# A two-layer graph kernel on one core: other orders for the first and last pairs, one load moved to another queue, filler products at the end left out

## The chip, the cores and the metric

The kernel runs on one core of one Trainium2 chip. A core has five engines, each with its own instruction stream: TensorE (PE in the profile, its weight loads apart as PEld), VectorE (DVE), ScalarE (ACT), GpSimd (POOL) and SyncE (SP, which here only issues DMAs). The metric is the device time in microseconds; less is better. Before the change the median of three runs is 2414.87 us (2414.79 to 2415.64).

## The reference

128 graphs of 128 nodes with 512 features each. Layer 0 is masked attention with 8 heads of 64, layer 1 a graph attention with one head; each is added to its input and layer-normalised. All in float32.

```python
# layer 0
q, k, v = x @ Wq + bq, x @ Wk + bk, x @ Wv + bv          # 8 heads of 64
logits = einsum('bqhd,bkhd->bhqk', q, k) / 8
attn = softmax(where(adj > 0, logits, -1e9), axis=-1)
x = layernorm(x + relu(einsum('bhqk,bkhd->bqhd', attn, v) @ Wo + bo))
# layer 1
Wh = x @ W
e = leaky_relu((Wh @ a1)[:, :, None] + (Wh @ a2)[:, None, :], 0.2)
x = layernorm(x + elu(softmax(where(adj == 0, -1e9, e), axis=2) @ Wh))
```

## The kernel before

Two graphs are worked on together, a pair; there are 64 pairs, 0 to 63. A pair's work is cut into some 130 steps. Each step is a small function that issues one to eight instructions, mostly on one engine, and has a key: `qk0`, `mask_logits1`, `edge_row`. A last digit 0 or 1 is the graph within the pair (or, for products, the number of the product). In this text a key with a point and a pair is one step: `qk2.1` is the step qk2 of pair 1.

The order of everything is written out by a plan. `PLAN` gives each key a due time, `PERIOD` (78.77) is added for each pair, and `ENDS` gives the first and last pairs shifts of their own on top; the units are the plan's own. `at` (in the main function) puts each step into a list with that sum, the list is sorted, and the steps are issued in this order. So a due time is no time on the chip: it only decides the place of a step's instructions in each engine's stream. An engine works its stream in order; a semaphore holds an instruction until its data are there or its buffer is free. The middle pairs have no shifts and so all have one order.

What the steps of a pair do, by stage:

- Loads, all on SP: `load_blocks` (x in a block form, four DMAs, two buffers), `load_x` (x once more for the residual, three buffers), `load_adj`. `x_transpose` (DVE) makes xT.
- Queries and keys, values, output and second-layer weights are each multiplied by a two-by-two block scheme with 7 products instead of 8: `qk0` to `qk6` (sixteen matmul rows of the profile each), `v0`..., `o0`..., `w0`... (four rows each). It needs sums of blocks: of the weights once at the start (`sums_qk`, `sums_v` on DVE, `sums_o`, `sums_w` on POOL), of the left side for each pair (`x_sums`, `o_sums`, `z_sums` on POOL). The products go to the three PSUM banks A, B and C, one buffer each, and several products are added up in one bank. Between two such products other engines read the bank: `_p1`, `_p1q`, `_c11` (ACT mostly) read A; `_p6`, `_p7`, `_c21` (DVE) read B; `_c22`, `_c12` (DVE) read C. The next product into a bank must wait for the read.
- Attention: `logits` (PE), `fill_logits` (POOL memset), `mask_logits`, `max_logits` (DVE), `exp_logits` (ACT, eight activations), `sum_logits` (DVE), `norm_logits` (ACT, eight), `weights_t` (DVE), then a turn through HBM: `weights_out` (tensor prd) and `weights_in` (prT), `mix_values` (PE, tile po), `mix_values_out` (ACT).
- First norm: `residual0x`, `stats0x`, `mean0x` (DVE), `rstd0x`, `shift0x` (POOL), `norm0x` (ACT).
- Second layer: `edge_termsx` and `edge_blocks` (DVE), `edge_row` (four DMAs, tile ejr), `edge_sums` (ACT), `edge_leaky`, `edge_mask`, `edge_max` (DVE), `edge_exp` (ACT), `edges_t` (DVE) and through HBM with `edges_t_out`, `edges_t_in` (tile attT), `mix_nodes` (PE, tile pz), `mix_nodes_out` (ACT), the w products, `elu_exp` (ACT), `elu_low` (POOL), `elu_max` (DVE), `residual1x` (POOL), the second norm, `store`.

The tiles po, pz, and the transposes named below share one PSUM buffer of tag "ps".

At the start, `a` (1024 numbers) is folded into W, since the second layer needs only W@a1 and W@a2. `fold_a(i)` (keys `sums_fold1`, `sums_fold0`) first issues a DMA on POOL's queue which spreads its half of `a` over all partitions, then does eight DVE multiplications with sums; `fold_t` (PE, tile pwa) transposes the result and `fold_out` (ACT) takes it out. Pair 0 does its queries and keys by plain products, `qk_plain`, since the weight sums aren't ready.

The last pair has no later work to overlap with. It turns its attention weights on PE, does its o and w products plainly from rows of the weights that are loaded again (`rows_o`, `rows_w`, into the buffers of the left sums), and does on DVE what POOL does elsewhere.

Products of zeros, or of the identity, that nobody reads keep PE at work: `keep_going` (12 at the very start) and `keep_going_late`, which `at` puts behind the steps named in `GOING`.

```python
GOING = {('o3', -1): 6, ('mix_nodes0', -2): 2, ('w3', -2): 5, ('w5', -2): 10, ('edges_t', -1): 3, ('mix_nodes1', -1): 1}
shift = ENDS.get(p if p < n_pair // 2 else p - n_pair, {}).get(key, 0.0)
events.append((p * PERIOD + PLAN[key] + shift, len(events), fn, args))
```

Of the kernel before, what the change touches and what calls it, by code (L numbers as in the profile page):

```python
# [8 lines left out]
F32 = mybir.dt.float32  # L9
# [10 lines left out]
    load_adj=-214.2762, load_blocks=-156.4567, sums_qk=-119.9046, x_transpose0=-118.9579, sums_v=-112.8775,  # L20
    x_transpose1=-64.055, sums_fold1=-60.5833, sums_fold_t1=-41.0724, sums_fold0=-37.6761, sums_fold_out1=-36.5398,
    qk0=-36.0224, x_sums=-35.8404, qk1=-32.9779, qk_p1=-31.7105, fill_logits0=-31.5232, sums_fold_t0=-29.2377,
    qk4=-28.6459, qk_p6=-28.5331, qk_p1q=-27.7049, qk2=-26.3155, qk_c11=-24.8916, qk3=-22.6254, v0=-21.402,
    qk_p7=-19.9439, qk_c22=-19.9339, qk5=-14.7467, qk6=-13.4439, qk_c21=-7.8856, qk_c12=-7.8498, v_p1=-4.7268,
    v1=-4.5449, fill_logits1=-1.8505, mask=-1.2435, v_p6=-0.2943, logits=0.0, sums_fold_out0=0.6684,
    mask_logits0=1.9952, max_logits0=3.7429, v3=4.4065, v_p7=4.433, v2=7.4467, v_c11=9.2069, v4=9.2085,
    mask_logits1=10.0374, load_x1=10.3213, v5=13.2871, v_c22=14.6665, exp_logits0=14.7511, v_c21=15.0921,
    v6=17.2266, v_c12=17.5754, max_logits1=22.1216, sums_o=22.3895, sum_logits0=24.0633, norm_logits0=27.409,
    exp_logits1=33.3029, weights_t0=43.7048, sum_logits1=43.7767, norm_logits1=52.0118, weights_out0=53.6197,
    weights_t1=55.6065, weights_out1=68.011, weights_in0=70.4393, weights_in1=74.301, mix_values0=75.8522,  # L30
    mix_values_out0=80.7212, mix_values1=81.4334, mix_values_out1=85.4398, load_x0=87.1711, sums_w=90.2554,
    o_sums=101.6394, o0=106.2181, o_p1=113.6365, o1=113.6652, o4=115.875, o_p6=116.2192, o_p1l=117.1503,
    o3=117.1603, o_p7=117.3205, o2=117.7709, o_c11=118.2449, o_c22=118.2872, o5=120.8539, o6=121.6955,
    o_c21=121.8792, residual01=122.7569, o_c12=122.7614, stats01=122.8191, mean01=123.8502, residual00=127.7304,
    rstd01=128.2803, shift01=128.7729, stats00=130.3078, norm01=131.2371, mean00=131.4538, rstd00=133.9815,
    edge_term01=134.3884, shift00=135.5918, edge_term11=137.3863, norm00=140.4496, edge_term10=144.2793,
    edge_blocks=146.1519, fill_edges=152.9599, edge_row=155.4786, edge_term00=159.9559, edge_sums=163.3873,
    edge_leaky=169.0665, edge_mask=174.9959, edge_max=179.2956, edge_exp=184.846, edges_t=185.9311,
    edges_t_out=188.282, edges_t_in=189.7663, mix_nodes1=211.95, mix_nodes_out1=218.2462, mix_nodes0=220.5122,
    mix_nodes_out0=222.7905, z_sums=231.0565, w0=248.2279, edge_norm=250.3865, w_p1=253.8429, w1=254.0225,  # L40
    w2=254.7456, w_p6=256.7486, w3=258.7144, w_c11=259.1252, w4=262.9461, w_p7=264.5461, w5=268.1992,
    w_c22=268.2862, w6=268.4953, w_c21=269.0061, w_c12=270.9016, elu_exp1=288.3615, elu_exp0=298.9658,
    elu_low1=307.1177, elu_max1=314.1197, elu_low0=326.1878, elu_max0=338.6625, residual10=340.2052,
    stats10=349.6362, mean10=349.9591, residual11=350.8328, rstd10=358.934, stats11=386.2458, mean11=395.8811,
    shift10=413.3316, rstd11=414.603, shift11=416.7025, finish0=436.5642, finish1=440.8676, store0=451.5942,
    store1=492.1186, tail_exp=492.2186, tail_max=492.3186, tail_sum=492.4186, tail_norm=492.5186)
# [3 lines left out]
        qk_p1=-693.3008, qk_p1q=-562.1962, qk_p6=-558.7086, qk0=-497.8592, x_transpose1=-494.0942,  # L50
        x_transpose0=-448.1221, fill_logits0=-367.3107, load_x1=-359.65, qk1=-335.4701, qk2=-331.5901,
        load_adj=-316.9328, load_blocks=-299.7933, qk_c11=-289.6601, tail_max=-280.732, mask=-257.6647, qk3=-220.34,
        fill_logits1=-212.9934, qk_c21=-211.3615, fill_edges=-182.6923, qk_c12=-180.0174, x_sums=-178.1562,
        logits=-170.7364, qk_c22=-165.6554, load_x0=-157.2757, qk5=-129.4956, exp_logits0=-115.2104,
        weights_out0=-114.1682, max_logits0=-113.2581, mask_logits1=-111.564, mask_logits0=-111.5243, v4=-108.9856,
        weights_t0=-107.8966, weights_in0=-106.3568, v1=-104.9602, v3=-103.5122, v_p6=-102.5092,
        sum_logits0=-99.1902, v_p1=-98.6495, v2=-98.1896, v_c22=-97.279, v_p7=-96.9685, v6=-95.93,
        max_logits1=-92.4852, v_c11=-92.0931, norm_logits0=-91.8454, v5=-91.0373, weights_t1=-89.8414, v0=-89.7163,
        norm_logits1=-87.923, sum_logits1=-87.4384, v_c12=-84.3643, exp_logits1=-84.0508, v_c21=-82.1213,
        weights_in1=-81.3671, weights_out1=-75.5973, mix_values0=-73.0572, o_sums=-72.5018,  # L60
        mix_values_out0=-71.3249, stats11=-70.0451, mix_values_out1=-68.3664, o0=-68.2642, mix_values1=-65.5116,
        o_p1l=-63.5095, o1=-61.1023, o_p1=-60.89, qk_p7=-54.0233, mean11=-52.6597, o2=-52.1908, o_p6=-51.8324,
        o3=-51.3338, o5=-49.9351, o_p7=-47.5345, o_c11=-46.8, o_c22=-46.5822, o6=-46.5728, residual11=-45.7167,
        o4=-45.2658, o_c21=-41.1905, store1=-37.7402, residual01=-37.493, elu_low0=-36.3281, residual00=-34.7161,
        stats01=-31.1527, stats00=-30.3568, o_c12=-30.2986, elu_low1=-29.8226, elu_exp0=-28.3417,
        edge_term10=-25.0922, norm00=-23.3134, mean00=-22.364, elu_exp1=-20.4366, elu_max1=-19.6739,
        shift00=-19.0277, rstd00=-18.0188, edge_max=-12.5663, edge_mask=-9.2627, edge_norm=-8.9206, mean01=-8.3685,
        w4=-8.2022, shift01=-8.0908, rstd01=-7.6618, mix_nodes1=-7.0678, edges_t=-6.1798, edge_exp=-5.696,
        edge_term00=-5.0867, edges_t_out=-4.9358, edge_leaky=-4.1925, mix_nodes0=-3.6711, mix_nodes_out1=-3.3264,
        w_c22=-2.764, w5=-2.6295, w6=-2.2085, w_p1=-1.9921, w_c21=-1.864, mix_nodes_out0=-1.4624, w_c12=-0.5349,  # L70
        w_p7=-0.4357, w1=-0.3674, edge_sums=-0.3649, finish1=-0.2784, edge_row=0.4769, w_p6=1.2165,
        edge_blocks=1.691, w_c11=1.7828, w3=2.1516, w0=2.4355, w2=2.5822, elu_max0=4.042, rstd11=4.5885,
        edge_term11=7.4074, norm01=8.5979, shift10=10.18, residual10=10.2246, edge_term01=10.4225, z_sums=13.5305,
        qk4=14.4327, edges_t_in=14.663, shift11=23.8601, stats10=33.5595, finish0=35.2453, store0=36.1082,
        rstd10=37.0667, mean10=39.7004, tail_exp=66.8184, tail_norm=66.9674, tail_sum=88.0048, qk6=88.4639),
    1: dict(
        tail_norm=-490.1808, tail_max=-153.045, load_x1=-116.7791, qk_p1q=-113.1873, qk0=-111.5532, qk_p1=-110.0434,
        qk4=-107.6095, qk2=-106.2391, qk3=-105.0977, x_sums=-102.7439, qk1=-102.1183, fill_logits0=-100.8075,
        qk_p6=-100.3165, qk_c11=-99.2056, qk_p7=-95.9145, v0=-95.2879, x_transpose1=-94.0568, v_p1=-93.2182,
        fill_logits1=-91.2167, qk5=-91.0325, qk_c22=-87.7854, qk_c21=-86.0555, mask=-83.9068, qk6=-74.9886,  # L80
        qk_c12=-72.8526, v1=-72.8444, max_logits1=-71.4972, v_p6=-70.6212, v4=-66.8154, v2=-66.3646,
        logits=-65.0664, mask_logits0=-65.0249, mask_logits1=-64.5572, v3=-63.432, exp_logits1=-63.0166,
        max_logits0=-62.096, v_c22=-61.3606, v_c11=-59.6449, v5=-58.7736, v_p7=-55.6045, elu_max0=-48.704,
        v6=-46.8286, v_c21=-46.2548, sum_logits0=-46.1168, residual10=-45.9116, elu_low0=-45.8965,
        exp_logits0=-45.0705, norm_logits0=-44.0432, v_c12=-37.6454, weights_in0=-36.7489, edge_norm=-35.6444,
        weights_t0=-34.4351, norm_logits1=-31.9896, x_transpose0=-30.4421, sum_logits1=-28.0582,
        weights_in1=-26.5576, weights_out1=-25.0926, o_p1l=-24.9338, o_p1=-23.9869, weights_out0=-23.5663,
        weights_t1=-23.4312, o2=-22.2075, mean11=-20.5856, o_sums=-20.3084, store1=-19.9954, elu_exp0=-19.6693,
        o3=-19.0271, o0=-18.871, o1=-18.228, o_p6=-18.1951, stats11=-17.7549, o_c11=-16.1903, load_x0=-16.0355,
# [153 lines left out]
def tile_two_graph_layers(ctx: ExitStack, tc: tile.TileContext, x, adj, wq, bq, wk, bk, wv, bv, wo, bo, w, a, out,  # L243
# [8 lines left out]
    nc = tc.nc  # L252
# [831 lines left out]
```

## Time and profile before

| | us |
|---|---|
| median of three runs | 2414.87 |
| the profiled execution | 2416.63 |
| its span, first to last instruction | 2414.8 |
| PE busy in the span | 2379.1 |
| one pair in the middle (from one qk step to the same of the next pair) | 36.73 |
| first qk product starts | 7.28 |
| `qk0.4` starts | 140.45 |
| last o product ends | 2376.7 |
| last matmul ends | 2406.8 |

The granted PE clock is 0.998 of full speed over the whole span. The sum of the changes is made against the profiled execution, 1.76 us above the median of the runs.

In a row of the timeline the numbers are start and duration in microseconds, then engine, line, operation, output<-inputs with the number of partitions and elements, a count, and in brackets the engine's idle time before the row with what ended it. In a row of waits: the total, how many, and the longest.

### The profile page before, as it was taken

The page shows a single profiled execution, that of the slowest core. Times are in us where ns is not written, and L with a number is a line of the kernel's source. Part 1 is how long each engine was busy: PE and PEld are TensorE (multiplying, and loading weights), DVE is VectorE, ACT ScalarE, POOL GpSimd, SP SyncE. Part 2 cuts the span into 40 slices and gives each one's busy share as a digit, 9 for nine tenths or more (in the row PEclk, how much of TensorE's full clock was granted, in tenths as well). Part 3 has the DMA queues.
Part 4 walks back from the last instruction along what each step waited for, and adds up shares of the span by engine and source line. Part 5 has one row for each costly group of instructions (what it writes and reads, how often), then busy time and mean ns, then how long its engine had stood idle before and what let it go on. Part 6 is the DMA issues. An engine that isn't in the chain of part 4 may idle for free.

```text
span 2414.8 us, 51884 instructions
## 1 busy us (share of the span) xinstructions
PE 2379.1 (99%) x17768; PEld 2147.7 (89%) x17768; DVE 1859.3 (77%) x3883; ACT 1557.8 (65%) x5512; POOL 1414.3 (59%) x1990
## 2 busy tenths in 40 slices
PE   8999999999999999999999999999999999999997
PEld 7889989989899899899899898998998998998885
DVE  5777777877877877777777778778778777777776
ACT  4656766766766666666667667666666666676664
POOL 3446665655556565665656555565566656555557
PEclk9999999999999999999999999999999999999999
DMA  8435445344344444454443443444444544534333
GB/s 194 114 67 130 112 105 131 101 118 123 104 123 116 112 123 115 101 134 109 108 132 101 117 123 103 123 117 112 123 115 101 134 110 108 134 98 116 109 85 81
DMA packets 341382, 276.59 MB, mean 115 GB/s; under 512 B 126400, under 2 KB 288960, under 8 KB 341120
## 3 DMA queue, kind: packets, MB, share of 16 engines
q1 hardware_dynamic: 339568, 271.17, 43.7%
q8 instruction: 142, 2.33, 0.4%
q10 hardware_dynamic: 1216, 1.31, 0.3%
q0 software_dynamic: 336, 0.79, 0.2%
q14 instruction: 120, 0.98, 0.1%
HBM read 156.90 MB, written 107.87 MB: 110 GB/s over the span
## 4 chain that ended last, share of the span: by engine, by line
PE 92%; DMA 3%; DVE 2%; ACT 2%; SPq 1%; issue 0%; POOL 0%; POOLq 0%; ACTq 0%; DVEq 0%
PE pBqk L486 14%; PE pCqk L486 9%; PE pAqk L486 9%; PE pBv L475 7%; PE pBo L475 7%; PE pBw L475 7%; PE po L804 5%; PE s L731 5%; PE pAo L475 4%; PE pz L914 4%; PE pCw L475 4%; PE pCo L475 4%; PE pAv L475 4%; PE pCv L475 4%; PE pAw L475 4%; DMA ejr<-ej 1%
## 5 line engine op out<-in xcount | busy, mean ns | idle before, releaser
L754 ACT ACTIVATE pr<-pr,nmax 128x128 f32<-128x128 f32 x1024 | 395.3, 390 | 4.0 <-DVE nmax L748 4.0
L763 ACT ACTIVATE pr<-pr,tot 128x128 f32<-128x128 f32 x1024 | 314.5, 411 | 49.8 <-DVE tot L758 49.6
L813 ACT ACTIVATE oT<-po,bv 128x128 f32<-128x128 f32 x512 | 145.0, 364 | 286.0 <-PE po L804 286.0
L956 POOL TENSOR_TENSOR cw<-cw,co 128x512 f32<-128x512 f32 x126 | 159.5, 1285 | 227.1 <-DVE cw L950 227.1
L513 POOL TENSOR_SCALAR rstd<-mv 128x1 f32<-128x1 f32 x255 | 97.6, 383 | 270.4 <-DVE mv L508 261.1
L945 POOL TENSOR_SCALAR t<-t 128x512 f32<-128x512 f32 x126 | 246.9, 1960 | 13.2 <-ACT t L941 13.1
L486 PE MATMUL pBqk<-sx,wqk 128*128 128x128 f32 x2016 | 245.6, 275 | 0.5 <-DVE tot L758 0.5
L486 PE MATMUL pCqk<-sx,wqk 128*128 128x128 f32 x2016 | 246.0, 275 | 0.0
L486 PE MATMUL pAqk<-xT,wqk 128*128 128x128 f32 x2016 | 245.5, 275 | 0.0
L486 PEld LDWEIGHTS pBqk<-sx,wqk 128*128 128x128 f32 x2016 | 239.8, 192 | 3.8 <-issue 0.6
L486 PEld LDWEIGHTS pAqk<-xT,wqk 128*128 128x128 f32 x2016 | 236.3, 192 | 7.0
L486 PEld LDWEIGHTS pCqk<-sx,wqk 128*128 128x128 f32 x2016 | 235.9, 192 | 0.2
L739 POOL MEMSET pr<- 128x1024 f32 x128 | 121.8, 953 | 134.4 <-DVE prb L773 129.8
L743 DVE COPY_PREDICATED pr<-mask,s 128x1024 f32<-128x1024 int32 x128 | 171.0, 1337 | 33.7 <-PE s L731 32.5
L835 DVE SCALAR_TENSOR_TENSOR scr<-co,wa_bc 128x512 f32<-128x512 f32 x256 | 186.3, 728 | 11.3 <-ACT co L523 5.7
L754 ACT ACTIVATION_READ_ACCUMULATOR pr<-pr,nmax 128x1 f32 x1024 | 193.8, 189 | 0.0
L773 DVE STREAM_TRANSPOSE prb<-pr 128x1024 f32<-128x1024 f32 x126 | 156.1, 1239 | 20.2 <-ACT pr L763 19.8
L514 POOL TENSOR_TENSOR rstd<-rstd,half 128x1 f32<-128x1 f32 x255 | 144.7, 567 | 21.2
L748 DVE TENSOR_REDUCE nmax<-pr 128x8 f32<-128x1024 f32 x128 | 155.3, 1213 | 0.2
L804 PE MATMUL po<-prT,cv 128*64 128x128 f32 x2048 | 140.2, 279 | 2.8 <-DMA prT<-prd 2.8
L919 ACT COPY zT<-pz 128x512 f32<-128x512 f32 x128 | 75.9, 593 | 100.8 <-PE pz L914 100.8
L475 PE MATMUL pBv<-wv,sx 128*128 128x256 f32 x512 | 138.0, 392 | 2.4 <-DVE u2v L679 1.3
(198 smaller groups left out, 5982.6 us busy)
## 6 DMA issues: line engine op xcount, KB each, us to landing
prd<-prb SPq DMA_DIRECT2D x126, 512.0 KB, 2.9
prT<-prd SPq DMA_DIRECT2D x504, 128.0 KB, 3.6
x<-in_x_dram SPq DMA_DIRECT2D x128, 256.0 KB, 4.2
out_dram<-cw SPq DMA_DIRECT2D x128, 256.0 KB, 3.6
xb<-in_x_dram SPq DMA_DIRECT2D x252, 128.0 KB, 4.0
adj<-in_adj_dram SPq DMA_DIRECT2D x64, 128.0 KB, 2.1
ejr<-ej SPq DMA_DIRECT2D x256, 32.0 KB, 3.9
atd<-atb SPq DMA_DIRECT2D x63, 128.0 KB, 1.8
```

What stands on the lines that cost most here:

```text
L475: nc.tensor.matmul(out, left_block(left, blk.pair, a_i, c), right_block(weight, b_i)[:, c, :], start=first and c == 0, stop=j in LAST and ...
L486: nc.tensor.matmul(out[:, f * P:(f + 1) * P], weight[:, b_i, c, f * P:(f + 1) * P], left_block(left, blk.pair, a_i, c), start=first and f ...
L743: nc.vector.copy_predicated(PR[b], MASK[p][:, i, :].unsqueeze(1).to_broadcast([P, H, P]), ST.pop(("s", b)).rearrange("p j h k -> p (j h) k"))
L748: nc.vector.tensor_reduce(NMAX[b], PR[b], AX.X, ALU.max, negate=True)
L754: nc.scalar.activation(PR[b][:, h, :], PR[b][:, h, :], AF.Exp, bias=nmax[:, h:h + 1], scale=1.0, accum_out=TOT[b][:, h:h + 1])
L763: nc.scalar.activation(PR[b][:, h, :], PR[b][:, h, :], AF.Copy, scale=tot[:, h:h + 1])
L773: nc.vector.transpose(PRB[b].rearrange("p k h s -> p h k s"), PR.pop(b).rearrange("p h (k r) -> p h k r", r=32))
L804: nc.tensor.matmul(ST["o", b][j * DH:(j + 1) * DH, hp, :], v[:, h * DH:(h + 1) * DH], prT[:, :, j * (H // 2) + hp, :], start=True, stop=True)
L813: nc.scalar.activation(OT[b][:, f, :], po[:, f, :], AF.Identity, bias=bv_sb[:, f:f + 1], scale=1.0)
L835: nc.vector.scalar_tensor_tensor(scr, X1[b], 1.0, wa_bc[s], op0=ALU.mult, op1=ALU.mult, accum_out=acc)
L945: side_engine(b // 2).tensor_scalar(t, t, 1.0, -1.0, op0=ALU.min, op1=ALU.add)
L956: side_engine(b // 2).tensor_tensor(Y[b], Y[b], X1.pop(b), op=ALU.add)
```

## The change

It has four parts.

1. `ENDS` has tables for nine pairs instead of seven: 0, 1, 2, 3 and -5, -4, -3, -2, -1 (counted from the end) in place of 0, 1, 2 and -4 to -1. All numbers in them are new. In `PLAN` the middle's numbers stay; only the ten `sums_` keys of the start have other due times. `PERIOD` and the numbers of buffers stay.
2. `a` is loaded once, with the weights, on SP's queue, into the buffer of the o sums. `fold_a` issues no DMA any more.
3. `GOING` is empty: of the products that nobody reads only the 12 at the start remain, 27 at the end are gone.
4. `qk_plain` takes its start and stop flags from which product of a bank comes first in the issue order, instead of fixing that to its number.

```diff
-GOING = {('o3', -1): 6, ('mix_nodes0', -2): 2, ('w3', -2): 5, ('w5', -2): 10, ('edges_t', -1): 3, ('mix_nodes1', -1): 1}
+GOING = {}
...
     load_rows(w_b, nc.sync, w)
+    a_bc = buf([P, 2, D], F32, "so", "a_bc")
+    nc.sync.dma_start(a_bc.rearrange("p i d -> p (i d)"), bass.AP(tensor=a.tensor, offset=a.offset, ap=[[0, P], [1, 2 * D]]))
...
     def fold_a(i):
-        a_bc = buf([P, D], F32, "t", f"a_bc{i}")
-        nc.gpsimd.dma_start(a_bc, bass.AP(tensor=a.tensor, offset=a.offset + i * D, ap=[[0, P], [1, D]]))
...
-                nc.vector.scalar_tensor_tensor(scr, right_block(w_b, blk)[:, c % 2, :], 1.0, a_bc[:, f * HALF:(f + 1) * HALF],
+                nc.vector.scalar_tensor_tensor(scr, right_block(w_b, blk)[:, c % 2, :], 1.0, a_bc[:, i, f * HALF:(f + 1) * HALF],
...
     def qk_plain(j):
-        if j == 0:
+        if ("qk", 0) not in BL:
...
+            b.started = ""
+        b = BL["qk", 0]
...
-            out = BL["qk", 0].bank[bank]
+            first = bank not in b.started
+            b.started += bank
...
-                                     left_block("x", 0, 2 * i + half, c), start=half == 0 and f == 0 and c == 0,
-                                     stop=half == 1 and f == NC - 1 and c == 1, skip_group_check=True)
+                                     left_block("x", 0, 2 * i + half, c), start=first and f == 0 and c == 0,
+                                     stop=not first and f == NC - 1 and c == 1, skip_group_check=True)
```

What the new tables do to the streams, at the places that the prediction speaks of (steps in the order in which the engine has them, before and after):

```
PE, pairs 0 and 1
  before  v0.0 v1.0 v4.0 v3.0 v2.0 v6.0 v5.0 qk0.1 qk4.1 qk1.1 qk2.1 qk3.1 sums_fold_t1 v0.1 sums_fold_t0 qk5.1 qk6.1 v1.1 mix_values0.0 logits.1
  after   v0.0 v1.0 v2.0 v3.0 v4.0 v6.0 v5.0 qk0.1 qk1.1 qk2.1 sums_fold_t1 qk4.1 qk3.1 v0.1 sums_fold_t0 qk5.1 qk6.1 v1.1 mix_values0.0 v3.1 logits.1
ACT, pairs 0 and 1
  before  v_c11.0 norm_logits0.0 qk_p1.1 qk_p1q.1 exp_logits1.0 qk_c11.1 sums_fold_out1 norm_logits1.0
  after   v_c11.0 norm_logits0.0 exp_logits1.0 qk_p1.1 qk_p1q.1 norm_logits1.0 qk_c11.1 sums_fold_out1
DVE, pair 0
  before  v_p6.0 mask_logits1.0 v_p7.0 v_c22.0 x_transpose1.1
  after   v_p6.0 x_transpose0.1 mask_logits1.0 v_p7.0 v_c22.0
SP, start
  before  load_blocks.2 load_x1.0 load_x0.0 weights_out0.0 load_adj.2 weights_in0.0 load_x1.1 weights_out1.0
  after   load_blocks.2 load_x1.0 load_adj.2 load_x0.0 load_blocks.3 weights_out0.0 load_adj.3 weights_in0.0 weights_out1.0
PE, pairs 2 and 3
  before  v1.3 mix_values0.2 logits.3 mix_values1.2 v3.3 v2.3 v4.3 v5.3 w0.0
  after   v2.3 mix_nodes0.0 v1.3 logits.3 mix_values0.2 v4.3 v3.3 mix_values1.2 v5.3 v6.3 w0.0
DVE, pairs 2 and 4
  before  edge_term10.2 qk_c21.4 qk_c12.4 edge_term11.2 edge_term01.2 edge_blocks.2 edge_term00.2
  after   edge_term10.2 edge_blocks.2 qk_c21.4 qk_c12.4 mask.4 edge_term00.2
PE, pairs 58 to 61
  before  v1.61 qk6.61 v2.61 mix_values0.60 logits.61 mix_values1.60 v3.61 w0.58 v4.61 v5.61
  after   v1.61 v2.61 v3.61 mix_values0.60 logits.61 mix_values1.60 v4.61 v5.61 w0.58 v6.61
ACT, pairs 59 to 61
  before  mix_values_out0.60 edge_sums.59 v_c11.61 mix_values_out1.60
  after   mix_values_out0.60 v_c11.61 mix_values_out1.60 w_p1.58 edge_sums.59
ACT, pairs 61 and 63
  before  edge_sums.61 v_c11.63 exp_logits0.63 mix_values_out1.62 w_p1.60 w_c11.60 edge_exp.61 exp_logits1.63
  after   edge_sums.61 mix_values_out1.62 edge_exp.61 w_p1.60 exp_logits0.63 w_c11.60 exp_logits1.63
ACT, pairs 62 and 63
  before  norm00.63 elu_exp0.61 mix_nodes_out0.62 w_p1.62 norm01.63 edge_sums.63
  after   norm00.63 mix_nodes_out1.62 finish1.59 norm01.63 mix_nodes_out0.62 elu_exp1.61 w_p1.62
DVE, pairs 61 to 63
  before  o_c11.63 residual00.63 stats00.63 mean10.60 mean00.63 stats11.60 o_c22.63 residual01.63
  after   o_c11.63 residual00.63 stats00.63 mean00.63 o_c22.63 residual01.63
  before  w_p7.62 elu_max0.61 edge_leaky.63 w_c22.62 w_c21.62 edge_mask.63
  after   w_p7.62 edge_term00.63 w_c22.62 elu_max0.61 edge_leaky.63 edge_mask.63
PE, pairs 62 and 63
  before  w1.62 w2.62 w4.62 w3.62 w5.62 w6.62 mix_nodes1.63 w0.63 mix_nodes0.63 w2.63
  after   w1.62 w4.62 w3.62 w2.62 w6.62 w5.62 mix_nodes1.63 mix_nodes0.63 w0.63 w2.63
```

## The prediction

> **What bounds the kernel now.** I read the page's busy shares first, then the windows by stretch of the run, then PE's waits, and last the timeline around each wait.
>
> ```profile
> PE 2379.1 (99%) x17768; PEld 2147.7 (89%) x17768; DVE 1859.3 (77%) x3883; ACT 1557.8 (65%) x5512; POOL 1414.3 (59%) x1990
> ```
>
> PE is busy 99% of the span, so only PE's idle time is for sale, 35.7 us in all. Where it lies, the windows tell (start:end, length, busy time of PE, PEld, DVE, ACT, POOL, clock, DMA share, GB/s):
>
> ```profile
> 40.00:50.00 10.00, 5.41 (x35) 4.98 (x35) 6.70 (x23) 4.91 (x15) 0.39 (x1) 0.81 0.37 88
> 50.00:60.00 10.00, 10.00 (x99) 9.07 (x99) 5.10 (x8) 1.61 (x6) 5.66 (x5) 0.85 0.77 183
> 1000.00:2000.00 1000.00, 1000.00 (x7552) 906.88 (x7551) 781.22 (x1632) 657.10 (x2328) 599.62 (x845) 1.00 0.45 116
> 2260.00:2280.00 20.00, 16.88 (x85) 14.31 (x84) 13.48 (x30) 10.89 (x43) 11.15 (x16) 1.00 0.34 87
> ```
>
> The middle has no idle PE at all. From 170 us to 2226 us the list of PE's waits is empty. Time won at the start therefore shifts the whole rest, and time won at the end shortens the end; nothing between can take it back, because the orders of pairs 5 to 58 differ by a few places at the edges only. PE's waits, in two stretches (0 to 200 us, then 2200 us to the end), total, times, longest:
>
> ```profile
> PE pwa L445 <- DVE wa_rep L439: 4.1, 1, 4.1
> PE po L804 <- DMA prT<-prd: 2.3, 2, 1.9
> PE pBw L475 <- DVE u2w L679: 1.8, 1, 1.8
> PE pAw L475 <- ACT cv L694: 1.8, 1, 1.8
> ...
> PE pAw L475 <- ACT cv L694: 2.6, 1, 2.6
> PE pBw L475 <- DVE u3w L701: 1.7, 1, 1.7
> PE pBv L475 <- DVE u3v L701: 1.3, 1, 1.3
> PE pBv L475 <- DVE qT L611: 1.1, 1, 1.1
> ```
>
> Each wait is short and comes once. The largest has a price beyond itself, as the timeline shows:
>
> ```profile
> 43.44 0.43 DVE L435 SCALAR_TENSOR_TENSOR wa_scr<-w,a_bc 128x256 f32<-128x256 f32 x1 [2.99 <-DMA a_bc<-in_L_gnn_a_dram]
> ...
> 47.95 1.09 PE L445 MATMUL pwa<-ident,wa_rep 128*128 128x128 f32 x4 [4.14 <-DVE wa_rep L439]
> 48.83 3.62 PE L486 MATMUL pBqk<-xT,wqk 128*128 128x128 f32 x16
> 52.24 2.29 PE L486 MATMUL pCqk<-sx,wqk 128*128 128x128 f32 x16
> ```
>
> The fold of `a` waits for its transfer, PE waits for the fold, and PE's clock falls: the same product takes 1.95 us elsewhere. At the end ACT works in order, so a norm whose shift POOL finished at 2381.84 waits for a copy that itself waits for PE:
>
> ```profile
> 2383.51 0.37 ACT L666 COPY e1aw<-pAw 128x256 f32<-128x256 f32 x1 [1.22 <-PE pAw L475]
> 2383.78 0.81 ACT L523 ACTIVATE co<-co,nmean,rstd 128x512 f32<-128x512 f32 x1
> ...
> 2391.03 2.39 PE L998 MATMUL keep_going<-ident 128*128 128x128 f32 x20
> 2393.88 1.10 PE L475 MATMUL pCw<-w,sz 128*128 128x256 f32 x4 [0.46 <-DVE cw L706]
> 2395.46 0.71 PE L891 MATMUL pat<-ident,at 128*128 128x128 f32 x2 [0.47 <-ACT at L876]
> ```
>
> **What the Trainium skill says.** "TensorE: Matmul & The Clock Gate", Part 1, What's actually happening: after about 3.4 us of idleness PE's clock is halved, and about 3.4 us of work bring it back. The trace agrees: a gap of 4.14 us did it (clock 0.81 and 0.85 above), one of 2.64 us at 2260 did not (1.00). The same page, Architectural detail: ACT and VectorE take their queues strictly in order; the norm above is a case. "DMA: Bandwidth & Descriptors", Issuing engines are not separate DMA queues: moving a DMA to another queue saves only issue time, the bytes share the 16 engines. No run here separates that.
>
> **The change part by part.** I write keys of the plan with their pair, e.g. qk2.1. PE's work is the same but for the 27 zero products, so the sum is one of gaps. I followed the new orders of the engines with the durations of this trace: qk product 1.79 us, half product 0.86, logits 1.99, mix_values 1.02, eight exps 3.2 with their reads (36.73 to 39.92), bias pair 1.15 + 1.17, DVE 128x512 0.7.
>
> *a with the weights.* Two POOL DMAs of 256 KB become one SP DMA of 512 KB behind w and ahead of four block loads and the first x. w lands about 32 (issue near 24, median 7.7); a some 1 to 2 us later. The first fold needs it at 35.5. The loads it goes ahead of are late by 512 KB at 297 GB/s, 1.8 us; their first user ran at 50.05, so nothing. Second fold: 3.0 us of DVE waiting go, PE's 4.14 go, and the slow clock goes: (1.09-0.60)+(3.62-1.95)+(2.29-1.95) = 2.5. Sum -6.6. The buffer taken is that of the o sums, first wanted near 58; the folds are done near 45.
>
> *Pairs 0 and 1.* v6.0 waits for a DVE add that now follows a transpose (0.7): +0.5. The wait of 0.45 at qk3.1 goes. New: exp_logits1.0 stands ahead of qk_p1.1 and qk_p1q.1 on ACT. It starts at 34.25, ends 37.45; the two bias reads of bank A end 39.75; qk2.1 must not write A before, and qk1.1 ends at 36.8. PE waits 3.1 (between 2.6 and 3.4), below the gap that cost a clock; if it does, +2.4. Behind PE's wait stand the second fold's transposes, uncritical now. Pair 0's mix_values then starts at 51.5 instead of 55.33: -3.6 in all.
>
> *Pairs 1 to 4.* Waits of 0.37 (prT) and 0.88 (cv) go; I find new ones of 0.4 at o4.0 and 0.45 at v5.2: -0.4. In pair 2 the waits of 1.92 (prT of 1.2) and 1.79 (u2w) go, as v4, v3 of pair 3 are put ahead of that mix_values and w_p1.0 ahead of its reader; new ones of 0.6 at v5.3 and v6.3: -3.1. sums_o and sums_w move forward on POOL (5.2 us each) into time where POOL waited (12.28 us before 49.6). In pair 4, w0.1 waited 1.75 behind an ejr transfer of 4.09 us; edge_blocks.2 now comes before two DVE adds: -1.5. On SP, weights_out0.0 now stands behind four issues of load_blocks.3 (2.1 us), whose buffer is free at 32.3, before the 35.5 when it is ready: nothing. mix_nodes1.1 is put 4 products earlier, and I find its attT only 1.6 us ahead of it. Start: -3.6-0.4-3.1-1.5 = -8.6. I take 2.0 off for what such a walk doesn't see (late transfers, slower DVE beside POOL, the 0.1 after every po): -6.6, between -10 and -3.
>
> *Pairs 59 to 63.* Up to the last o product the waits are 0.23+0.31+2.64+0.48+1.06+0.24+1.33+0.17+0.58+0.49 = 7.5. v2 and v3 go ahead of mix_values and logits, v_c11.61 ahead of edge_sums.59 (which waits for an ejr transfer), edge_exp.61 ahead of exp_logits0.63: these aim at those very waits. I find 0.3 at v5.63 again. With 2.7 kept for others: -4.5.
> Then the chain from the last o product (end 2376.7) to the end, 38.1 us, which no other work fills. o_c22.63 began 0.96 late behind two statistics that now follow; norm01.63 waited 1.9 behind w_p1.62, which now follows it; edge_mask.63 waited 0.6 behind w_c22.62 and w_c21.62. That is 3.5; mix_nodes0.63 ahead of w0.63 hides one zT copy (0.6). Against it elu_low of 2 us each on POOL hold elu_max0.61 ahead of edge_leaky.63: I take -2.7.
>
> *Zeros.* 7.0 us of PE time that lay in idleness (sum of the keep_going rows from 2376 on); taking them away frees nothing. What they covered: PE now works about 8 us in 15 before the last 8 us of products. Cost of cold clock: nothing to 3.4; I take 1.0.
>
> Sum: -6.6-4.5-2.7+1.0 = -12.8. The profiled execution took 2416.63 (span 2414.8 and 1.8 around it) and would take 2403.8; the median of the runs, 1.76 below it, would be 2402.1.
>
> **Rivals.**
> 1. The clock falls in both new places: 2402.1+2.4+2.4 (3.4 less the 1.0 taken) = 2406.9. For: 3.1 us is near the 4.14. Against: 2.64 cost nothing.
> 2. The end keeps its length: pair 61's and 62's ejr and attT transfers (4.43 and 1.78 us in the chain of waits) set it whatever the order. -6.6 remains of the start: 2408.3; with the start at its weak end, 2411.9, no change. For: the chain of waits from 2328 on runs over prd, ejr, attT, not over PE. Against: those DMAs are issued after DVE steps that are moved forward.
> 3. Slower: eight exps ahead of a reader that frees a bank, as in pair 1, 3.1 us each. Place: ACT in the first four and last five pairs. One such wait is in my sum; four more, 12.4, eat the gain, a fifth makes it slower, and with six more the time is 2402.1+18.6 = 2420.7. For: ACT in order and single banks A, B, C. Against: in the others I walked, the bias reads were done 1 to 2 us before PE wanted the bank.
> That the change doesn't do what it says is no rival: the first products' start flags go by bank, but their order is unchanged.
>
> **How the numbers follow.** Forecast 0.52 (own range 2396 to 2407), rival 1 0.13, rival 2 0.22 (half of it no change), rival 3 0.13 (a tenth of the rest no change). 0.2% is 4.8 us, about what can be told from no change. Faster 0.52+0.13+0.11 = 0.76, same 0.12, slower 0.12. The range, 2395 to 2413, takes in the weak start and rival 2 and leaves rival 3 out.
>
> **What would show it.** Right: no a_bc row among DVE's waits, clock 1.00 from 40 to 60, the first mix_values near 51.5, qk0.4 near 133 instead of 140.45; a PE wait near 3 us at 37 to 40 behind ACT; the row of pat 17 us or less after the last pBo_last row instead of 18.8. Wrong: a clock below 1 near 40 or 2390, waits on po or pz for DMA above 1 us, or a PE wait over 2 us in the last five pairs.

## The result, and the profile after

| | before | after |
|---|---|---|
| median of four runs, us | 2415.26 | 2398.61 |
| range, us | 2414.79 to 2417.95 | 2397.80 to 2403.08 |
| ratio, 95% interval | | 0.9933 (0.9915 to 0.995) |
| the profiled execution, us | 2416.63 | 2403.08 |
| its span, us | 2414.8 | 2401.3 |
| `qk0.4` starts, us | 140.45 | 132.03 |
| last o product ends, us | 2376.7 | 2359.4 |
| from there to the end of the span, us | 38.1 | 41.9 |

The kernel is 0.67% faster. (A fourth run of before, 2417.95, came with those of after.) The profiled execution is the slowest of the four of after and gained 13.5 us in span; the median gained 16.65. The page of after, share of busy time (engine, us, share of the span, instructions):

```profile
PE 2376.6 (99%) x17714; PEld 2146.5 (89%) x17714; DVE 1864.7 (78%) x3883; ACT 1556.0 (65%) x5512; POOL 1408.9 (59%) x1988
```

PE's idle time fell from 35.7 us to 24.7. How far each pair is ahead is read from the first row of its logits, taken from the timeline of PE of each kernel and subtracted from the kernel before (us; minus is earlier):

| pair | 0 | 1 | 2 | 3 | 4 | 5 | 6 to 48 | 49 to 57 | 58, 59 |
|---|---|---|---|---|---|---|---|---|---|
| after | +0.64 | -2.69 | -2.91 | -4.89 | -8.38 | -10.51 | -10.65 to -10.69 | -10.3 | -10.0 |

The value of pair 1 understates the gain: in the new order one more product, v3.1, stands ahead of these logits (see the streams above). At the first mix_values, which comes before it in both orders, the gain is 3.74 us (55.33 to 51.59).

So 10.7 us come from the start, the middle gives back 0.7 in two short waits, and by the end of the last o product 17.3 are won. Behind it 3.8 are lost again. The windows of after show where (start:end, length, busy time of PE, PEld, DVE, ACT, POOL, clock, DMA share, GB/s):

```profile
30.00:40.00 10.00, 7.31 (x49) 6.95 (x50) 9.53 (x30) 9.09 (x39) 3.96 (x6) 0.93 1.13 240
40.00:50.00 10.00, 10.00 (x80) 9.85 (x79) 6.69 (x20) 3.99 (x13) 2.15 (x2) 0.90 0.33 113
...
2340.00:2360.00 20.00, 18.64 (x100) 12.13 (x99) 15.98 (x34) 10.22 (x27) 16.27 (x23) 1.00 0.32 81
2360.00:2380.00 20.00, 14.07 (x48) 10.57 (x47) 11.97 (x29) 8.18 (x17) 13.70 (x19) 0.74 0.30 69
2380.00:2402.00 22.00, 11.92 (x40) 8.39 (x40) 10.78 (x26) 8.00 (x14) 13.26 (x20) 0.73 0.24 92
```

The clock is below 1 in two places, around 40 us and from 2360 us on. PE's waits of after from 20 to 200 us (total, times, longest); the kernel before had eight groups there, 12.9 us together:

```profile
PE pAqk L536 <- ACT e1bqk L616: 2.1, 1, 2.1
PE pCv L525 <- DVE cv L759: 0.7, 1, 0.7
PE pBqk L536 <- POOL rstd L563: 0.4, 1, 0.4
```

The timeline of PE, first one row of before, then after at the first place and at the second:

```profile
55.33 1.09 PE L804 MATMUL po<-prT,cv 128*64 128x128 f32 x16
```

```profile
34.13 1.95 PE L536 MATMUL pBqk<-sx,wqk 128*128 128x128 f32 x16
38.22 3.54 PE L536 MATMUL pAqk<-xT,wqk 128*128 128x128 f32 x16 [2.14 <-ACT e1bqk L616]
...
51.59 1.09 PE L857 MATMUL po<-prT,cv 128*64 128x128 f32 x16
...
2359.39 1.03 PE L525 MATMUL pCw<-w,sz 128*128 128x256 f32 x4
2362.56 1.65 PE L967 MATMUL pz<-attT,co 128*128 128x128 f32 x8 [2.14 <-DMA attT<-atd]
2364.94 2.08 PE L967 MATMUL pz<-attT,co 128*128 128x128 f32 x8 [0.73 <-ACT zT L972]
2367.69 2.08 PE L525 MATMUL pAw<-w,zT 128*128 128x256 f32 x4 [0.68 <-ACT zT L972]
2369.56 1.91 PE L525 MATMUL pBw<-w,sz 128*128 128x256 f32 x4
...
2379.16 0.71 PE L944 MATMUL pat<-ident,at 128*128 128x128 f32 x2 [1.51 <-ACT at L929]
```

At 38.22 the product that usually takes 1.95 us takes 3.54: the clock fell in a wait of 2.14 us, and 1.6 us were lost beside the wait. At 2362.56 another wait of 2.14 us does the same, and the w products behind it take 1.9 to 2.1 us instead of 1.03. The row of pat starts 19.8 us behind the last o product; before it was 18.8.

### The profile page after: what moved, and what is told of

The parts are those of the page before. It is cut to its first block, busy times and chain, and to the rows that moved or that the text cites. A ratio compares the mean times of both kernels' runs of the same rounds, so it can differ in the third digit from the quotient of the medians.

```text
span 2401.3 us, 51762 instructions
## 1 busy us (share of the span) xinstructions
PE 2376.6 (99%) x17714; PEld 2146.5 (89%) x17714; DVE 1864.7 (78%) x3883; ACT 1556.0 (65%) x5512; POOL 1408.9 (59%) x1988
## 4 chain that ended last, share of the span: by engine, by line
PE 96%; ACT 1%; DMA 1%; DVE 1%; POOL 0%; issue 0%; SPq 0%; ACTq 0%; POOLq 0%; DVEq 0%
PE pBqk L536 14%; PE pAqk L536 9%; PE pCqk L536 9%; PE pBv L525 7%; PE pBw L525 7%; PE pBo L525 7%; PE po L857 5%; PE s L784 5%; PE pz L967 5%; PE pAo L525 4%; PE pAv L525 4%; PE pCv L525 4%; PE pCw L525 4%; PE pAw L525 4%; PE pCo L525 4%; ACT pr L807 1%
## 5 line engine op out<-in xcount | busy, mean ns | idle before, releaser
L967 PE MATMUL pz<-attT,co 128*128 128x128 f32 x1024 | 138.9, 280 | 4.8 <-ACT zT L972 2.2
L967 PEld LDWEIGHTS pz<-attT,co 128*128 128x128 f32 x1024 | 132.0, 195 | 9.4 <-ACT zT L972 3.1
```

What stands on the lines that cost most here:

```text
L967: nc.tensor.matmul(ST["z", b][:, c, :], X1[b][:, c * P:(c + 1) * P], attT, start=True, stop=True)
```

## The experiments

Each kernel is compared with the kernel before on the same chip. There the kernel before had a median of 2416.29 us beside start alone, end alone, a alone and the first run of the idle products; 2414.80 beside the changed kernel's second run, the kernel before without idle products, the reads first and the 12 products in the wait; and 2414.89 beside the rest.

**1. Start alone and end alone.** The changed kernel with the tables and idle products of the end as before, and the kernel before with the changed end.

```diff
 ENDS = {
     0: dict(...), 1: dict(...), 2: dict(...), 3: dict(...),
-    -5: dict(...), -4: dict(...), -3: dict(...), -2: dict(...), -1: dict(...),
+    -4: dict(...), -3: dict(...), -2: dict(...), -1: dict(...),
 }
-GOING = {}
+GOING = {('o3', -1): 6, ('mix_nodes0', -2): 2, ('w3', -2): 5, ('w5', -2): 10, ('edges_t', -1): 3, ('mix_nodes1', -1): 1}
```

> The changed kernel with the tables of the last pairs and the idle products of the kernel before: only the start is new. If start and end add up: the start's share is what stands constant between pairs 6 and 48, 10.65 us, so the time is 2404.2 to 2405.2, and the stretch from the last pBo_last row to the end is 38 us as before. Rival (part of the start's gain is lost at the end, because transfers there come at another time against the work): 2406.5 or more.

Measured: 2406.28 us (2404.61 to 2408.29), ratio 0.9962 (0.9949 to 0.9974). The shift is -11.05 in the middle; the last stretch is 38.2 us, as before. The times of the expectation stand on a kernel before of 2415.26, and on this chip it had 2416.29. The gain is 10.0 where the first theory has 10.65: what the start wins arrives at the end.

> The kernel before with the changed tables of the last five pairs and without the 27 idle products: only the end is new. If start and end add up: the median is lower by 16.65 - 10.65 = 6.0 us, so 2409.3 (2408.5 to 2410.5); before the last pBo_last row 7 us are won, and behind it 1 to 4 are lost, the more the lower the clock there. Rival (the end's gain needs the new start): 2412 or more.

Measured: 2408.32 us (2405.32 to 2409.84), ratio 0.9968 (0.9957 to 0.998): 8.0 us less, 2.0 more than I expected. Start and end together give 18.0; the change as a whole gave 16.65, and 15.1 when it was measured again. Within what the intervals allow, they add up. The end doesn't need the new start. In its profile the last stretch is 37.7 us, hardly shorter than the 38.1 of before and without any of the 27 products: attT came sooner here (PE waited 0.51 us for it), and the clock fell later and for fewer rows than in after:

```profile
2374.65 1.97 PE L498 MATMUL pAw<-w,zT 128*128 128x256 f32 x4 [1.15 <-ACT zT L942]
...
2388.53 2.08 PE L937 MATMUL pz<-attT,co 128*128 128x128 f32 x8 [0.68 <-ACT zT L942]
```

**2. a alone.** The kernel before, with a loaded once on SP behind w.

```diff
     load_rows(w_b, nc.sync, w)
+    a_bc = buf([P, 2, D], F32, "so", "a_bc")
+    nc.sync.dma_start(a_bc.rearrange("p i d -> p (i d)"), bass.AP(tensor=a.tensor, offset=a.offset, ap=[[0, P], [1, 2 * D]]))
...
-        a_bc = buf([P, D], F32, "t", f"a_bc{i}")
-        nc.gpsimd.dma_start(a_bc, bass.AP(tensor=a.tensor, offset=a.offset + i * D, ap=[[0, P], [1, D]]))
```

> The kernel before with one thing changed: a is loaded once, on SP behind the weights. Theory (my term for it: 3.0 of VectorE's wait, 4.14 of PE's wait and 2.5 of slow clock go, 6.6 together): qk0.4 starts near 133.9 instead of 140.45, the clock is 1.00 from 40 to 60 us, the time is 2408 to 2409.5. Rival (the wait moves: the fold is then held by something else, or PE has another gap of 2 us behind the exps there): qk0.4 starts at 136.5 or later, and the time is 2411.5 or more.

Measured: 2412.48 us (21 runs), ratio 0.9987 (0.998 to 0.9994), 3.8 us less. Both theories hold in part. The logits of pair 1 go from +0.34 (pair 0) to -6.05, so the fold is worth the 6.4 us of the first. At pair 2 the shift is -4.55. The timeline of PE of this kernel, two rows:

```profile
53.85 1.09 PE L804 MATMUL po<-prT,cv 128*64 128x128 f32 x16 [1.48 <-DMA prT<-prd]
...
2257.65 2.02 PE L475 MATMUL pAw<-w,zT 128*128 128x256 f32 x4 [2.48 <-ACT cv L694]
```

The first row is the give-back: PE is now early, and `mix_values1.0` waits 1.48 us for a transfer that was hidden before. The second row is another thing. The kernel before has the same wait in the same order, with a clock that stays up (its timeline of PE):

```profile
2262.81 1.13 PE L475 MATMUL pAw<-w,zT 128*128 128x256 f32 x4 [2.64 <-ACT cv L694]
```

In this profile the clock fell after 2.48 us of waiting, in that one it did not after 2.64. My estimate that PE's new waits would be free of it rested on that one row of before.

**3. The idle products.** First the changed kernel with the 27 products put back, twice, and the changed kernel itself once more; then the kernel before without them.

```diff
-GOING = {}
+GOING = {('o3', -1): 6, ('mix_nodes0', -2): 2, ('w3', -2): 5, ('w5', -2): 10, ('edges_t', -1): 3, ('mix_nodes1', -1): 1}
```

Put back, the first time:

> The changed kernel with the 27 idle products at the end put back. Theory (the last chain is 41.9 us long in the changed kernel, against 38.1 before, because PE falls to a clock of 0.73 to 0.74 in the last 40 us): the clock from 2360 on is 0.9 or more, pCw and pBw rows take about 1.1 us and not 1.9, the stretch from the last pBo_last row to the end is 37 to 39 us, and the time is 2394 to 2397, with less spread between its runs than the 5 us of the changed kernel. Rival (the stretch is longer because of the new order there: POOL's elu_low, attT transfers): the clock rises, but the stretch stays above 41 us and the time is 2398 to 2399.

Put back, the second time:

> The changed kernel with the idle products at the end, once more and unaltered, beside the two others of this set. Theory (at the wait of 2.15 us PE's clock falls in some executions only): qk2.1 takes 2.0 or 3.5 us, the shift from the first pair to pair 5 -12.7 or -11.1, and the time is 2394 to 2397 and within 1.5 us of the six-product kernel. Rival (the first time this kernel had luck, and the idle products are worth less than 3 us): 2397.5 or more.

The changed kernel again:

> The changed kernel once more, nothing altered, on the chip on which the others of this set run. Theory (PE's clock falls by chance in waits of 2 us): the wait at qk2.1 is again 2.1 to 2.2 us; qk2.1 takes either 2.0 or 3.5 us; the clock in the last 40 us differs from the 0.73 to 0.82 of the first profile, and the stretch behind the last pBo_last row lies between 37 and 42 us; its times spread over 3 us or more, around 2399. Rival (the clock follows from the program alone): the same rows slow as in the first profile, the stretch 41.5 to 42.3 us, a spread of 1.5 us or less.

The kernel before without them:

> The kernel before without its 27 idle products at the end, nothing else. Prediction's term: what they covered costs nothing to 3.4 us, 1.0 taken. Theory (a gap of 2 us behind the last o product is enough to lower PE's clock for several us, and more gaps follow): the stretch from the last pBo_last row to the end grows from 38.1 to 40 to 42 us, rows of pAw and pBw take 1.9 to 2.1 us in places, and the time is 2 to 4 us above the kernel before. Rival (the idle products lie in idleness and cost or save nothing): the same within 1 us, the stretch 38 to 39 us.

Measured:

| kernel | idle products | median, us | ratio to before (interval) | last stretch in the profile, us |
|---|---|---|---|---|
| after, first and second time | none | 2398.61, 2399.67 | 0.9933 (0.9915 to 0.995), 0.9936 (0.9923 to 0.9948) | 41.9, 39.8 |
| after, with them, twice | 27 | 2395.55, 2396.03 | 0.9916 (0.9903 to 0.993), 0.9924 (0.9911 to 0.9936) | 36.7, 37.8 |
| before | 27 | 2414.80 | 1 | 38.1 |
| before, without them | none | 2418.95 | 1.0015 (1.0008 to 1.0021) | 41.2 |

In the old order they are worth 4.15 us (1.9 to 5.1 by the interval); in the new one the medians of all nine runs each are 2399.07 and 2396.03, so 3.0. The intervals of the single ratios overlap in the new order, but of the nine runs with the products only two lie above the lowest of the nine without.

That 3.0 can hold some luck. At qk2.1, more than 2300 us ahead of these products, both profiles of after lost 1.6 us to the clock and neither profile with the products did; two other kernels with them (start alone, and the one with a on POOL's queue) lost it as well, so it is not the products that prevent it. Of the difference between the profiles 2.3 to 2.6 us stand at pair 20 already. In the last stretch they differ by 2.0 to 5.2 us, and the end alone had 37.7 us there without the products. The 21 runs against 25 in the old order are the firmer evidence. The window of the kernel with the products, second time, and its timeline of PE:

```profile
2360.00:2380.00 20.00, 17.08 (x101) 14.00 (x102) 12.40 (x26) 9.52 (x21) 16.26 (x17) 1.00 0.30 73
```

```profile
2356.14 1.50 PE L1051 MATMUL keep_going<-ident 128*128 128x128 f32 x12
2357.48 1.03 PE L525 MATMUL pCw<-w,sz 128*128 128x256 f32 x4
2358.35 1.05 PE L967 MATMUL pz<-attT,co 128*128 128x128 f32 x8
2360.13 1.16 PE L967 MATMUL pz<-attT,co 128*128 128x128 f32 x8 [0.73 <-ACT zT L972]
...
2362.99 1.03 PE L525 MATMUL pBw<-w,sz 128*128 128x256 f32 x4
...
2373.97 0.72 PE L944 MATMUL pat<-ident,at 128*128 128x128 f32 x2 [1.09 <-ACT at L929]
```

The clock is 1.00 where after had 0.74, pBw takes 1.03 instead of 1.91, and pat comes 17.8 us behind the last o product (16.7 the first time). The kernel before without its products shows the reverse in its timeline of PE:

```profile
2377.21 1.13 PE L914 MATMUL pz<-attT,co 128*128 128x128 f32 x8 [1.71 <-DMA attT<-atd]
...
2388.72 2.07 PE L475 MATMUL pBw<-w,zT 128*128 128x256 f32 x4 [2.83 <-DVE u3w L701]
2392.54 2.04 PE L475 MATMUL pCw<-w,sz 128*128 128x256 f32 x4 [1.74 <-DVE cw L706]
```

In the old order the theory of the clock stands. The rival of the second look at after, that the clock follows from the program alone, fails. The rows from the first pz to pBw are slow in both profiles. But behind pat the rows of pz and pAw_last took 2.08 and 2.81 us in the first (clock 0.73 there), and in the second:

```profile
2382.51 1.16 PE L967 MATMUL pz<-attT,co 128*128 128x128 f32 x8 [0.68 <-ACT zT L972]
2383.51 1.88 PE L706 MATMUL pAw_last<-rows_w,zT 128*128 128x512 f32 x4
```

And the mean clock of each run of after goes with its time:

| mean clock of the run | times of after, both sets, us |
|---|---|
| 0.998 | 2397.14, 2397.57, 2397.80 |
| 0.997 | 2398.14, 2399.07 |
| 0.996 | 2399.67, 2400.65, 2401.16 |
| 0.995 | 2403.08 |

With the idle products eight of nine runs have 0.999 and one 0.998. So after's spread, and the slow profiled execution, go with the clock. The products at the end don't secure it everywhere: the kernel before has them and spreads more widely (25 runs, 2411.83 to 2420.55, at 0.995 to 0.999).

**4. The wait at `qk2.1`.** Three kernels, all with the idle products at the end. In the first the two bias reads of bank A stand ahead of the eight exps on ACT; in the others 12 or 6 idle products lie in the wait.

```diff
     0: dict(
...
-exp_logits1=-105.4285,
+exp_logits1=-104.9029,
...
     1: dict(
-        qk_p1q=-111.8967,
+        qk_p1q=-122.7637,
...
-qk_p1=-109.3704,
+qk_p1=-118.8581,
```

> The changed kernel with the idle products at the end put back, and with the two bias reads of bank A of pair 1 ahead of the eight exps of graph 1 of pair 0 on ScalarE. Theory (the wait of 2.15 us at qk2.1 is nothing but those exps standing ahead of the reads): PE's wait there is 0.5 us or less, qk0.4 starts 1.8 to 2.2 us earlier than with the idle products alone (there 127.4 by the shift of its logits rows), and the time is 0.991 less 0.0008 of the kernel before, 2393 to 2394. Rival (the exps now start 3.3 us later, and prT of graph 1 comes later to mix_values1.0): PE waits 2 us or more at the second po or at another place before 70 us, and the time is 2395 or more.

Measured: 2396.15 us (2395.51 to 2397.44), ratio 0.9923 (0.991 to 0.9937). No gain: the rival holds, by a path that neither named. The timeline of PE:

```profile
34.22 1.95 PE L536 MATMUL pBqk<-sx,wqk 128*128 128x128 f32 x16
36.65 2.05 PE L536 MATMUL pAqk<-xT,wqk 128*128 128x128 f32 x16 [0.48 <-ACT e1bqk L616]
39.06 0.65 PE L495 MATMUL pwa<-ident,wa_rep 128*128 128x128 f32 x4 [0.36 <-DVE wa_rep L489]
...
44.84 0.63 PE L495 MATMUL pwa<-ident,wa_rep 128*128 128x128 f32 x4 [0.29 <-DVE wa_rep L489]
...
49.99 1.09 PE L857 MATMUL po<-prT,cv 128*64 128x128 f32 x16
...
54.92 1.09 PE L857 MATMUL po<-prT,cv 128*64 128x128 f32 x16 [0.79 <-PE s L784]
```

From the start of qk1.1 to the first mix_values it is 15.77 us; with the exps ahead it was 15.83 (33.16 to 48.99 in the second run with the idle products). The wait shrinks from 2.15 to 0.48, and the 1.6 won are given back at three places. The first fold isn't done any earlier, so its transpose starts 0.5 us later, counted from the row before it; v0.1 starts 0.3 later, behind a read of bank A on ACT (42.26 to 43.37); and the second fold's transpose 0.55 later, because the exps end later, DVE's reciprocal of their sums waits 0.67 for them, and the second fold stands behind that reciprocal in DVE's stream. Then `mix_values1.0` starts 0.79 late.

```diff
-GOING = {('o3', -1): 6, ...
+GOING = {('qk1', -63): 12, ('o3', -1): 6, ...
```

With 12:

> The changed kernel with the idle products at the end put back, and 12 more of them (1.5 us) behind qk1.1, in the wait of 2.15 us. Theory (in that wait the clock falls in some executions and not in others, and where it falls 1.6 to 1.75 us are lost): qk2.1 takes 1.95 to 2.05 us, the clock is 1.00 from 30 to 50 us, and the time is level with the idle products alone where those runs had no fall (0 to 1 us less). Rival (the idle products hold back qk2.1, whose bank was already free): qk2.1 starts later by 0.3 us or more against the end of the reads, and the time is 0.5 to 1.5 us more.

With 6:

> As the kernel with 12 products in the wait at qk2.1, with 6 of them: 12 rows, 1.4 us, since each product is two rows and 12 took 2.84 us against a wait of 2.15. Theory (12 held qk2.1 back by some 0.5 us, 6 do not; and they keep the clock): qk2.1 starts as soon as the reads of bank A are done, 4.1 us after qk1.1 starts, takes 1.95 to 2.05 us, and the shift of the logits rows from the first pair to pair 5 is -12.5 to -13 (with 12 it was -12.2, in the changed kernel -11.1, where the clock fell); the time is level with the idle products at the end alone, 0 to 1 us less. Rival (products of zeros in the gap don't hold the clock, or cost the same): qk2.1 takes 3 us or more, shift -11.5 or less.

Measured: with 12, 2398.37 us (2397.80 to 2400.52), ratio 0.9935 (0.9922 to 0.9947); with 6, 2396.13 us (2394.85 to 2396.65), ratio 0.9921 (0.9909 to 0.9934). The timelines of PE, with 12 and with 6:

```profile
35.59 2.84 PE L1051 MATMUL keep_going<-ident 128*128 128x128 f32 x24
38.27 1.95 PE L536 MATMUL pAqk<-xT,wqk 128*128 128x128 f32 x16
```

```profile
35.30 1.50 PE L1051 MATMUL keep_going<-ident 128*128 128x128 f32 x12
37.73 2.05 PE L536 MATMUL pAqk<-xT,wqk 128*128 128x128 f32 x16 [0.93 <-ACT e1bqk L616]
```

Each product is two rows, which I had missed, so 12 of them take 2.84 us and hold qk2.1 back; that was a size of mine. Part of the 12-product time has another cause: its profile has one wait of 1.3 us in the middle, near pair 8, that no other profile has. Six products fit, and qk2.1 takes 2.05 us. They save nothing against the same kernel without them (2396.03), whose clock did not fall there in either profile. That they keep the clock is thus not shown.

**5. The queue of a.** As the kernel with idle products, with the load of a issued by POOL at the start.

```diff
-    nc.sync.dma_start(a_bc.rearrange("p i d -> p (i d)"), ...
+    nc.gpsimd.dma_start(a_bc.rearrange("p i d -> p (i d)"), ...
```

> The changed kernel with the idle products at the end put back, and the one load of a issued on POOL's queue at the start instead of on SP's behind w. In the kernel before POOL issued the second half of a only at 36.45 us, behind a memset that waited, and it landed 7 us later. Theory (what cost the fold its 3.0 us and PE its 4.14 was the moment of the issue, not the queue): a lands before 25 us, the fold does not wait, qk0.4 starts as with SP's queue within 1 us, and the time is 2394.5 to 2397. Rival (the queue counts: on POOL's queue a goes ahead of the weights and takes 1.8 us of transfer from them): the first products wait longer before 20 us, every pair is 1 to 2 us later from the first logits on, and the time is 2397 to 2398.

Measured: 2401.94 us (2399.22 to 2402.55), ratio 0.9945 (0.9932 to 0.9959); 5.9 more than with SP's queue on the same chip. The timeline of PE, first of this kernel, then of the one with SP's queue:

```profile
9.46 2.91 PE L610 MATMUL pAqk<-xT,wqk 128*128 128x128 f32 x16 [2.79 <-DMA wqk<-in_L_gnn_Wq_dram]
...
40.98 3.68 PE L536 MATMUL pAqk<-xT,wqk 128*128 128x128 f32 x16 [2.15 <-ACT e1bqk L616]
```

```profile
6.88 2.02 PE L610 MATMUL pAqk<-xT,wqk 128*128 128x128 f32 x16 [0.75 <-DMA wqk<-in_L_gnn_Wq_dram]
...
37.26 2.05 PE L536 MATMUL pAqk<-xT,wqk 128*128 128x128 f32 x16 [2.15 <-ACT e1bqk L616]
```

a is issued at 1.5 us and lands 7.2 us later; the fold doesn't wait, as the theory said, but the first product starts 2.6 us later, behind the weights, PE has a low clock (0.91 up to 20 us, against 1.00), and the first logits are 3.7 us behind. The rival holds, and it costs more than it said. From pair 1 on the profile is 5.4 us behind, because the clock fell at qk2.1 here and not there (1.6 us more behind the same wait). That happened in other kernels as well and isn't shown to come from the queue. So the profiles give 3.7 us to the early transfer, and whether the rest of the 5.9 is its doing stays open. "DMA: Bandwidth & Descriptors", Issuing engines are not separate DMA queues, in the Trainium skill, says that transfers of all queues share the same 16 engines; this run agrees. When a's bytes move is then what matters: behind w and ahead of the fold. A load on POOL's queue at that later time was not run, so the queue by itself is untested.

## Why the prediction was right, and where not

The time was 2402.1 forecast and 2398.61 measured, within its range. The sign and most of the mechanism were right: short waits of PE go at both ends, and the middle keeps the gain. Several sizes were off, and that the sum came so near is partly luck. For the profiled execution, on which it was made, 2403.8 was forecast and 2403.08 measured: up to pair 59 the gain was 10.0 instead of 6.6, in the last pairs 7.3 instead of 4.5, and the rest, forecast 1.7 shorter, became 3.8 longer. The median is lower still because after's profiled execution is its slowest run, 4.5 above the median, where 1.76 was assumed.

**a, -6.6.** Right: 6.4 in the kernel with a alone. That 1.5 of it would be lost at the next transfer when a moves alone was not in the sum; in the whole change the new orders avoid that wait.

**Pairs 0 and 1, -3.6.** The first mix_values came at 51.59 against the 51.5 of the text. (From 55.33 that is 3.8 earlier, not 3.6, and the terms listed add up to 3.45; the slip is small.) Pair 0's own logits were 0.64 late, so the step gave 4.4. Errors cancelled. "PE waits 3.1 ..., below the gap that cost a clock" had the wait too long by 1.0 and the clock wrong: it fell and cost 1.6. With a clock that stayed up, the two profiles with idle products show -6.0 for this step. The reason given, that 2.64 us cost nothing, was one row; the same wait cost a clock in another run. And one wait was left out of the sum. Of PE's rows in pair 0's v products the first here is before, the second after:

```profile
28.76 1.10 PE L475 MATMUL pBv<-wv,sx 128*128 128x256 f32 x4 [1.34 <-DVE u2v L679]
```

```profile
30.55 1.10 PE L525 MATMUL pCv<-wv,sx 128*128 128x256 f32 x4 [0.72 <-DVE cv L759]
```

The 0.72 is v6.0, 0.5 more than before, as forecast. But the new order, with v2.0 ahead of v3.0, also takes away the wait of 1.34 at v3.0. Where +0.5 stood in the sum, PE gained 1.0.

**Pairs 1 to 4, -5.0 less 2.0.** Measured -6.9 (from -3.74 at the first mix_values to -10.65). The step that failed is "I find new ones": the waits of 0.4 at o4.0, 0.45 at v5.2 and 0.6 at v5.3 and v6.3 are not in after's list, which has one wait of 0.4 from 54 to 170 us. The 2.0 taken off on top for late transfers wasn't needed either.

**The middle.** "Nothing between can take it back" held but for 0.7 us in two waits.

**Pairs 59 to 63, -4.5.** Measured -7.3 (from -10.0 at pair 59 to -17.3). Before's waits of 7.5 are nearly all gone; the 2.7 kept for new ones was the mis-sized term.

**The final chain, -2.7.** Too much. In the two profiles with idle products the stretch is 36.7 to 37.8 us against 38.1, so the new order is worth 0.3 to 1.4. Steps that each begin earlier do not add up here: in the new order pCw waits 0.9 for POOL's rstd and pz still waits 0.73 and 0.45 for the copy of zT.

**Zeros, +1.0 of 0 to 3.4.** Too little: 4.15 in the old order and about 3.0, luck included, in the new. I had counted what they covered and not that a wait of 1 to 2 us behind other short waits can be enough for the clock; with the end alone 1.15 us did it, behind waits of 0.51 and 0.73.

So rival 1 came true in mechanism, in both its places, without its time of 2406.9, because the pairs at both ends gave about 7 us more than the sum had. All three signs that the text called wrong appeared as well: a clock below 1 near 40 and 2390, and a wait of pz for its transfer of 2.1 us, which is also a wait of PE over 2 us in the last five pairs. pat came at 19.8 us, not at 17; with the idle products 16.7 and 17.8. Rival 2's mechanism is in that same wait for attT, which was 0 to 0.9 us in the profiles with idle products, where six of them (1.5 us) stand ahead of it, and 0.5 to 2.4 in those without. Rival 3 is one place of ACT and no more.

The best of all is then the new order with the old idle products: 2395.55 and 2396.03 us in two sets, 18.9 to 20.7 below the kernel before, about 3 below the changed one.

## What to carry to other kernels

An order that removes PE's short waits at the ends is worth their sum, if a wait that replaces them is looked up in the new trace rather than allowed for; but a wait that is taken from PE shows only its first successor, and the next one (here a fold on DVE, a turn through HBM) may take all of it back. Products that nobody reads cost nothing as long as they fit into the wait, and their worth is the clock of the work behind, so it must be measured by removing them, not by what they cover, and over many runs, since one execution can keep the clock by luck. Where a load is late, ask when its bytes move and what they displace before asking which queue issues them.

## What was not expected of the hardware

The length of one wait doesn't tell whether PE's clock falls. Waits of 2.14 to 2.16 us at qk2.1 were followed by a fall in four profiles and not in two; at another step, near 2260, 2.48 us did at once and 2.66 us a product later, while 2.35 and 2.64 us did not, each in one profile. "TensorE: Matmul & The Clock Gate", Part 1, What's actually happening, in the Trainium skill, says that activity is judged in windows that run freely, not from a kernel's start, which agrees with a fall that comes and goes between runs; its about 3.4 us of idleness don't agree with falls after 2.14 us, and the measurement decides. In the six profiles at qk2.1 the wait began at 35.1 us where the clock stayed and at 35.7 us or later where it fell. Whether that is a rule or chance six profiles can't say, and it was not tried.
